# Attention's score rounds back to back, and values' products summed outside the PSUM banks

## The chip, the cores and the metric

The kernel runs on one NeuronCore of a Trainium2 chip. The metric is device time in microseconds (us) of one execution. TensorE (PE) multiplies matrices and writes to PSUM, eight banks of 128 partitions by 512 fp32. VectorE (DVE), ScalarE (ACT) and GpSimd (POOL) work elementwise; the first two read PSUM, and in this kernel GpSimd reads and writes SBUF alone. SyncE (SP) issues the transfers.

## The reference

The program computes two transformer layers, L0 and L1, in fp32 on x of shape (4, 512, 320), with a context of shape (4, 1601, 192). Each layer is

```
h1 = layernorm(x);  x = attention(h1, h1) + x         # 512 keys
h2 = layernorm(x);  x = attention(h2, context) + x    # 1601 keys
h3 = layernorm(x);  a, g = split(h3 @ ff_w1 + ff_b1)
x = (a * gelu(g)) @ ff_w2 + ff_b2 + x
```

where attention has 20 heads of 16 columns:

```
q, k, v = x @ wq, ctx @ wk, ctx @ wv      # per head
a = softmax(q k^T * 16**-0.5)             # over the keys
out = (a v, heads side by side) @ wo + bo
```

## The kernel before

**Units.** The work is cut into units. An attention unit is one layer, one kind (self or cross), one of the four batches and one group of four heads: 20 self units and 20 cross units per layer, 80 in all. A feed-forward unit ("ff") is one layer and batch. Units are in the order self, cross, ff. Keys are taken in chunks of 128: four in a self unit, 13 in a cross unit (the last has 65 keys), so there are 680 chunks.

**A chunk.** The function `main` works on one unit. For each head of a chunk, `score` multiplies the transposed keys (`kT`, 32 partitions per head: 16 of the head, one that adds the negated maximum, the rest zero) by the queries with their maxima (`qT`), into a bank `st` of 128 keys by 512 queries. ScalarE takes the exponential of it into a tile `pr` in SBUF. `values` then multiplies `pr` by the values (`vals`, 16 columns and a column of ones, 17 in all, so that the softmax's sum comes out as well). The four heads' products stand at partitions 0, 32, 64 and 96 of one bank, `av`, and are summed over the unit's chunks inside that bank. After the last chunk ScalarE copies `av` to a tile `o`, and `divide` transposes it and divides by the sums.

**Maxima.** The maxima over the keys must be known before a unit starts. `max_pairs` multiplies queries and keys once more the other way round (`sps`), and VectorE reduces each bank to one column (`pm`, or `nmax` where there is just one stretch of keys). `max_reduce` and `max_end` put these together: the latter transposes the maxima and adds them to the queries, which makes `qT`. Maxima of the next two units are worked on while the current one runs: `give` hands out which.

**Rounds.** A matmul of a score or of a maximum has 32 rows, so four of them with different heads go side by side on TensorE. `round_of` issues two scores (heads 0 and 1, or 2 and 3) and two maxima of the other two heads. A chunk has an even round (heads 0 and 1) and an odd one (2 and 3). An fp32 matmul shows as two passes in the profile, so a round is eight MATMUL lines there.

**Steps.** All other work of TensorE is cut into steps, which wait in queues ("chains"): projections of queries, keys and values (`qps`, `kps`, `vps`), the output projection (`ops`), and transposes of normalised rows, context, divided output and undivided output (`hps`, `cps`, `aps`, `dps`). Projections use columns in tiles of 32, as the values' products do; transposes use the whole array. Each step has a cost, a due round and a test of readiness. `steps` runs between rounds: a credit grows each round by the pace that the queues need, and `pick` takes the step with the earliest due round, shifted by `late_by`. Steps of the cost `LIGHT` are work of VectorE alone. A clock counts rounds. The program's order on each engine is what this planning issues; the engines then run it in order and wait for each other by semaphores.

**Order in a chunk before.** Even round; the values of the chunk before (`flush`); steps. Odd round; steps. So something nearly always stands between two rounds.

**Banks.** Three banks `st` for scores in a ring, four banks `m` for maxima and for steps, one bank `av`. The exponentials' tiles `pr` are a ring of eight in SBUF.

**GpSimd.** `to_slots` spreads keys and queries to their 32-partition slots, in two instructions of GpSimd per step; GpSimd also computes the normalisation's inverse root and adds the output bias to x.

Of the kernel before, what the change touches and what calls it, by code (L numbers as in the profile page):

```python
# [9 lines left out]
F32 = mybir.dt.float32  # L10
I32 = mybir.dt.int32
AF = mybir.ActivationFunctionType
ALU = mybir.AluOpType
# [5 lines left out]
H, DH = 20, 16  # L19
# [40 lines left out]
def kernel(ctx: ExitStack, tc: tile.TileContext, x, context, ws, out):  # L60
# [14 lines left out]


    nc = tc.nc
    dma = nc.sync.dma_start
# [7 lines left out]
    dram = ctx.enter_context(tc.tile_pool(name="dram", bufs=1, space=bass.MemoryType.DRAM))  # L86
    ps_st = ctx.enter_context(tc.tile_pool(name="ps_st", bufs=3, space=PSUM))
    ps_m = ctx.enter_context(tc.tile_pool(name="ps_m", bufs=4, space=PSUM))
    ps_av = ctx.enter_context(tc.tile_pool(name="ps_av", bufs=1, space=PSUM))
    ctx.enter_context(tc.manual_schedule())  # L90
# [13 lines left out]

    vals = const.tile([P, NC2, H, VW], F32, name="vals")
    nc.gpsimd.memset(vals, 1.0)

# [19 lines left out]

    av = ps_av.tile([P, N], F32, name="av")
    nc.vector.memset(av, 0.0)


    xs = [const.tile([P, NQ, D], F32, name=f"x{b}") for b in range(B)]

    def load_x(b):
# [4 lines left out]

    wq1, wk1, wv1, wq2, wo1, wo2 = (  # L140
        wpool.tile([P, 3, D], F32, name=n) for n in ("wq1", "wk1", "wv1", "wq2", "wo1", "wo2")
    )
    wk2, wv2 = (wpool.tile([P, 2, D], F32, name=n) for n in ("wk2", "wv2"))
# [35 lines left out]
    def load_self(l):  # L179
        load_norm(l, 0)  # L180
        load_rows(wq1, ws[l]["q1"], DK)
        load_rows(wk1, ws[l]["k1"], DK)
        load_rows(wv1, ws[l]["v1"], DK)
        load_rows(wo1, ws[l]["o1_w"], DK)

    def load_cross(l):
        load_norm(l, 1)
        load_rows(wq2, ws[l]["q2"], DK)
        load_rows(wk2, ws[l]["k2"], CK)
        load_rows(wv2, ws[l]["v2"], CK)  # L190
        load_rows(wo2, ws[l]["o2_w"], DK)

# [68 lines left out]
    chains = {n: deque() for n in ("divide", "project", "norm", "context", "early", "proj", "values")}  # L261
    clock = {"round": 0, "credit": 0.0, "light": -1, "side": None, "odd": False}
    ALIKE = ("project", "early", "proj", "values")
# [25 lines left out]
    def late_by(n):  # L289

        if not clock["side"]:
            return 0
        cost = sum(chains[n][0][0])
        if clock["side"] == "self":
            return 3 if n not in ALIKE else 1 if cost < 0.85 else 0
        return 4 if n in ALIKE and cost < 0.7 else 0

    def pick():  # L300
        heads = [
            (q[0][1] + (late_by(n) if clock["odd"] else -late_by(n)), n)
            for n, q in chains.items()
            if q and q[0][2]() and q[0][3]() and (q[0][0][0] != LIGHT or clock["light"] < clock["round"])
        ]
        return min(heads)[1] if heads else None
# [24 lines left out]

    def steps(odd, whole=False, spent=0.0):


        clock["credit"] = max(-2.0, min(4.0, clock["credit"] + pace()))
        clock["side"] = None if odd is None else "self" if whole else "cross"
        clock["odd"] = bool(odd)
        done = 1 if spent else 0
        while True:
            name = pick()  # L340
            if name is None:
                break
            cost = sum(chains[name][0][0])
            if cost >= 0.1:
                credit = clock["credit"]
                if odd is None:
                    enough = credit >= (3.0 if done else 0.5 * cost)
                elif odd:
                    enough = not done or credit >= (3.0 if done > 1 else 2.0)
                else:  # L350
                    enough = credit >= (3.0 if done > 1 else 1.5 if done else 0.5)
                if not enough:
                    break
                done += 1
            run(name)
            if cost == LIGHT:
                clock["light"] = clock["round"]
        clock["side"] = None
        clock["round"] += 1

# [418 lines left out]
    def add_finish(u):  # L779
# [29 lines left out]
        def project(t, part):  # L809
            wo = wo2 if u.cross else wo1  # L810
            cols = slice(part * D // 2, (part + 1) * D // 2)
            ps = step_bank([P, 512], "ops")
            for k, at, n in DK:
                for f, m in tiles_of(P):
                    nc.tensor.matmul(  # L815
                        ps[f : f + m, : D // 2],
                        lhsT=held["outT"][:n, k, t * P + f : t * P + f + m],
                        rhs=wo[:n, k, cols],
                        start=(k == 0),
                        stop=(k == 2),  # L820
                    )
            nc.vector.tensor_tensor(xs[u.b][:, t, cols], ps[:, : D // 2], xs[u.b][:, t, cols], ALU.add)

        r = clock["round"]
        add("divide", 0.58, divide, r + 4, yes, lambda: clock["round"] > r)
        if u.g == G - 1:
            for k, at, n in DK:
                add(
                    "divide", 0.58, lambda k=k, at=at, n=n: turn(k, at, n), r + 6 + k,
                    lambda: not chains["project"],  # L830
# [12 lines left out]

            add("divide", 0.0, end, r + 8)

# [14 lines left out]
    def main(u, give, nxt):  # L860
# [3 lines left out]
        def score(c, j, pool=ps_st, tag="st"):  # L864
# [12 lines left out]
            return exponential  # L877

        def values(c):
            r = min(P, u.nkeys - c * P)  # L880
            if u.g in (0, 2):
                until(lambda: units[u.i - u.g].vmade[u.g // 2] > c, "values")
            for j, i in enumerate(HEAD):
                nc.tensor.matmul(  # L884
                    av[i * SLOT : i * SLOT + VW, :],
                    lhsT=vals[:r, c, u.g * HG + i, :],
                    rhs=pr.pop((c, j))[:r, :],
                    start=(c == 0),
                    stop=(c == u.nch - 1),
                )  # L890
            u.valued = c + 1
            if c == u.nch - 1:
                u.o = one.tile([P, N], F32, tag="o", name="o")
                nc.scalar.copy(u.o, av)
                add_finish(u)

        halves = 2 * u.nch
        for h in range(halves):
            c, odd = divmod(h, 2)
            rounds = []  # L900
            if nxt is None or nxt.kind == "ff":

                if not odd:

                    round_of(
                        [
                            lambda j=j, ring=ring: score(c, j, *ring)
                            for j, ring in zip(range(HG), ((ps_st, "st"), (ps_m, "m")) * 2)
                        ],
                        [],  # L910
                    )
            else:
                pair, rounds = give(h)
                round_of([lambda j=j: score(c, j) for j in ((2, 3) if odd else (0, 1))], pair)
            if odd:
                u.scored = c + 1
                late.append(lambda c=c: values(c))
            else:
                flush()
            ends = h == halves - 3 and nxt is not None and nxt.kind != "ff"  # L920
            if ends:
                max_end(nxt)
            if rounds or ends:
                clock["light"] = clock["round"]
            if odd:
                steps(True, not u.cross, 0.6 if ends else 0.0)

            start["quad"] = True
            for i, extra in enumerate(rounds):
                if i and next_cost() is not None:  # L930
                    run(pick())
                round_of([], extra)
            start["quad"] = False
            if h == halves - 4 and nxt is not None and nxt.kind != "ff":
                max_reduce(nxt)
                clock["light"] = clock["round"]
            if not odd:
                steps(False, not u.cross)

# [20 lines left out]
    def ff_main(u, give, nxt):  # L960
        done = 0

        def beside(room, n):
# [6 lines left out]
            if done == u.steps - 1 and nxt is not None and nxt.kind != "ff":  # L970
                max_reduce(nxt)
                max_end(nxt)
            steps(None)
            for _ in range(n - 1):
                steps(None, spent=9.0)

# [71 lines left out]
    def after(u):  # L1048
# [4 lines left out]
        if u.b == B - 1 and u.l + 1 < L:  # L1053
            {"self": load_self, "cross": load_cross, "ff": load_ff}[u.kind](u.l + 1)

    def left(v):
# [20 lines left out]
    def giver(u):  # L1077
# [14 lines left out]
        def give(h, alone=False):  # L1092
# [6 lines left out]
            for v in ahead:  # L1099
                total += left(v)  # L1100


                rest = v.start - (7 if alone else 3) - clock["round"]
                if rest > 0:
# [4 lines left out]
            while owed >= 1.0 and any(left(v) for v in ahead) and not (alone and rounds and rest > -4):  # L1109
                hand = [v for v in ahead if left(v) and all(q and at_hand(v, q) for q in v.pairs)]  # L1110
                if not hand and ahead[0].start - 3 - clock["round"] > 1:
                    break
# [15 lines left out]
    load_x(0)  # L1128
    load_self(0)
    load_bias(0, 0)  # L1130
    load_bias(0, 1)
# [72 lines left out]
```

## Time and profile before

The median of three runs is 3605.57 us (3605.49 to 3605.57).

| what | value |
|---|---|
| time of the profiled execution | 3605.48 us |
| its span in the profile | 3603.7 us |
| granted TensorE clock | 1.0 |
| 0 to 45 us (loads, first unit's preparation) | TensorE busy 41.46 us |
| 400 to 1490 us (cross-attention of layer 0) | TensorE busy 1089.71 us, DVE 698.58, ACT 637.53, POOL 245.60 |
| 1490 to 1820 us (mostly feed-forward) | TensorE busy 327.81 us, DVE 80.91, ACT 75.48 |
| score matmuls, line 868 | 5440 passes, 637 ns mean |
| maxima matmuls of 512 keys, line 718 | 5120 passes, 639 ns mean |
| values' matmuls, line 884 | 5440 passes, 598 ns mean |
| exponentials, line 874 | 2720, 595 ns mean |
| copies of `av`, line 894 | 80, 586 ns mean |
| maxima reductions, line 726 | 2560, 685 ns mean |

A line of a group shows the line number of the kernel, the engine, the operation, the tile written and the tiles read, the shape and the count; then the busy time and the mean of one, and the idle time in front of it with what ended that. A line of the timeline shows start, duration of the merged instructions, and what they are. Four matmuls that lie side by side are each counted as busy, and the passes' durations overlap, so TensorE's speed is read from starts and not from durations. PEld is its weight load, which may lie beside a matmul.

### The profile page before, as it was taken

What the parts mean: (1) busy time and instruction counts of PE and PEld (TensorE: products, weight loads), DVE (VectorE), ACT (ScalarE), POOL (GpSimd) and SP (SyncE); (2) the same over time, 40 slices, a digit from 0 to 9 for tenths busy, and PEclk for the clock granted to TensorE, in tenths of its full rate; (3) what the DMA queues carried; (4) which work ended last, traced back from release to release, by engine and by line L of the source; (5) the groups of instructions that cost most, each with busy time, mean ns of one, the idle gap of its engine ahead of it and who ended that gap; (6) DMA issues with size and microseconds to landing.
All of it is one profiled execution on the core that took longest, in us unless ns stands there. A gap on an engine that the chain in (4) does not pass through costs nothing.

```text
span 3603.7 us, 80038 instructions
## 1 busy us (share of the span) xinstructions
PE 3590.4 (100%) x34386; PEld 1479.2 (41%) x34386; DVE 2037.6 (57%) x3699; ACT 1816.0 (50%) x3665; POOL 794.7 (22%) x1676
## 2 busy tenths in 40 slices
PE   9999999999999999999999999999999999999999
PEld 4344443343343343254443444433433333333455
DVE  7665756666666666422256657566666666664221
ACT  4555455655655655611135554556555555556110
POOL 3323321212311312011122233212222222210100
PEclk9999999999999999999999999999999999999999
DMA  4000000000000000000020000000000000000000
GB/s 126 2 10 18 15 11 4 27 2 3 28 2 2 26 2 6 7 1 7 1 70 2 2 3 2 2 15 2 2 15 2 1 15 1 2 1 1 8 8 15
DMA packets 32106, 41.87 MB, mean 12 GB/s; under 512 B 11780, under 2 KB 30216, under 8 KB 30472
## 3 DMA queue, kind: packets, MB, share of 16 engines
q1 hardware_dynamic: 31752, 36.76, 3.6%
q8 instruction: 270, 4.42, 0.5%
q14 instruction: 84, 0.69, 0.1%
HBM read 29.21 MB, written 7.54 MB: 10 GB/s over the span
## 4 chain that ended last, share of the span: by engine, by line
PE 99%; DVE 0%; ACT 0%; issue 0%; DMA 0%; SPq 0%; DVEq 0%
PE st L868 37%; PE av L884 19%; PE fps L986 8%; PE sps L718 5%; PE vps L666 5%; PE kps L618 5%; PE yps L1021 5%; PE ops L815 3%; PE qps L593 3%; PE fps L998 2%; PE sps L733 2%; PE dps L785 1%; PE mps L773 1%; PE hps L427 1%; PE aps L806 1%; PE cps L506 0%
## 5 line engine op out<-in xcount | busy, mean ns | idle before, releaser
L874 ACT ACTIVATE pr<-st 128x512 f32<-128x512 f32 (+1 forms) x2720 | 1472.4, 595 | 1084.9 <-PE sps L718 907.6
L726 DVE TENSOR_REDUCE pm<-sps 128x1 f32<-128x512 f32 x1920 | 1234.2, 685 | 672.1 <-PE sps L718 672.1
L868 PE MATMUL st<-qT,kT 32*128 32x512 f32 (+1 forms) x5440 | 1558.8, 637 | 1.3 <-ACT pr L874 1.3
L718 PE MATMUL sps<-kT,q 32*128 32x512 f32 x5120 | 1467.0, 639 | 0.2 <-DVE kT L542 0.2
L884 PE MATMUL av<-pr,vals 128*17 128x512 f32 (+1 forms) x5440 | 720.1, 598 | 0.0
L868 PEld LDWEIGHTS st<-qT,kT 32*128 32x128 f32 (+1 forms) x5440 | 441.3, 180 | 618.4 <-issue 478.3
L548 POOL TENSOR_SCALAR kT<-kst,keep,ones 64x200 f32<-64x200 f32 (+2 forms) x796 | 413.1, 519 | 629.1 <-ACT kst L628 391.6
L726 DVE TENSOR_REDUCE nmax<-sps 128x1 f32<-128x512 f32 x640 | 409.5, 685 | 246.5 <-PE sps L718 245.3
L548 POOL TENSOR_SCALAR q<-qst,keep,zero 64x128 f32<-64x128 f32 (+1 forms) x476 | 230.2, 484 | 1408.5 <-ACT qst L605 1375.8
L718 PEld LDWEIGHTS sps<-kT,q 32*128 32x128 f32 x5120 | 426.3, 183 | 29.8 <-DVE pm L726 9.5
L884 PEld LDWEIGHTS av<-pr,vals 128*17 128x17 f32 (+1 forms) x5440 | 92.1, 95 | 493.2 <-issue 484.9
L986 PE MATMUL fps<-hT,w 128*128 128x512 f32 x640 | 287.2, 597 | 0.0
L1004 ACT ACTIVATE gl<-fps,b 128x512 f32<-128x512 f32 x80 | 54.8, 687 | 384.9 <-PE fps L998 384.9
L986 PEld LDWEIGHTS fps<-hT,w 128*128 128x128 f32 x640 | 117.2, 190 | 141.9 <-issue 138.5
L666 PE MATMUL vps<-wv,ctxT 96*32 96x192 f32 (+2 forms) x3264 | 153.3, 302 | 0.0
L666 PEld LDWEIGHTS vps<-wv,ctxT 96*32 96x32 f32 (+1 forms) x3264 | 91.4, 109 | 137.6 <-issue 62.1
L618 PE MATMUL kps<-ctxT,wk 96*32 96x200 f32 (+1 forms) x2560 | 140.8, 338 | 0.0
L593 PE MATMUL qps<-hT,wq 112*32 112x128 f32 (+3 forms) x2880 | 129.3, 311 | 2.0 <-ACT hT L434 2.0
L815 PE MATMUL ops<-wo,aT 112*32 112x160 f32 (+1 forms) x3072 | 130.2, 302 | 0.0
L674 ACT COPY vals<-vps 128x128 f32<-128x128 f32 (+3 forms) x272 | 80.2, 295 | 89.3 <-PE vps L666 88.5
L1005 DVE SCALAR_TENSOR_TENSOR hid<-fps,b,gl 128x512 f32<-128x512 f32 x48 | 35.9, 750 | 156.0 <-ACT gl L1004 153.7
L815 PEld LDWEIGHTS ops<-wo,aT 112*32 112x32 f32 (+1 forms) x3072 | 90.8, 110 | 75.2 <-issue 42.8
(80 smaller groups left out, 2074.6 us busy)
## 6 DMA issues: line engine op xcount, KB each, us to landing
ctxT<-ctxT SPq DMA_DIRECT2D x8, 1200.8 KB, 6.9
w<-in_L_xattn_ff_w_dram SPq DMA_DIRECT2D x4, 1280.0 KB, 9.5
ctxin<-in_ctx_dram SPq DMA_DIRECT2D x24, 192.0 KB, 2.5
w<-in_L_xattn_ff_w_dram SPq DMA_DIRECT2D x2, 1600.0 KB, 11.9
out_dram<-x SPq DMA_DIRECT2D x16, 160.0 KB, 1.8
x<-in_x_dram SPq DMA_DIRECT2D x3, 640.0 KB, 9.4
w1r<-in_L_xattn_ff_w_dram SPq DMA_DIRECT2D x4, 320.0 KB, 11.0
wq<-in_L_xattn_q_dram SPq DMA_DIRECT2D x8, 140.0 KB, 2.7
```

The costliest lines, as they stand in the source:

```text
L548: nc.gpsimd.tensor_scalar(to, stage[rows, :w], keep[b][rows], more[rows], ALU.mult, ALU.add)
L593: nc.tensor.matmul(ps[to, :w], lhsT=wq[:n, k, gs], rhs=first.hT[:n, k, at[i] : at[i] + w], start=(k == 0), stop=(k == 2),)
L618: nc.tensor.matmul(ps[to, :w], lhsT=wk[:n, k, gs], rhs=first.kvT[:n, k, c0 : c0 + w], start=(k == 0), stop=(k == len(u.kck) - 1),)
L666: nc.tensor.matmul(ps[f : f + m, at : at + w], lhsT=u.kvT[:n, k, c * P + f : c * P + f + m], rhs=wv[:n, k, h0 * DH : h1 * DH], start=(k == 0),
L718: nc.tensor.matmul(ps, lhsT=u.q[j * SLOT : (j + 1) * SLOT, t * P : (t + 1) * P], rhs=u.kT[j * SLOT : (j + 1) * SLOT, u.k0 + s * 512 : u.k0 ...
L726: return lambda: nc.vector.tensor_reduce(to, ps, AX.X, ALU.max, negate=(ns == 1))
L815: nc.tensor.matmul(ps[f : f + m, : D // 2], lhsT=held["outT"][:n, k, t * P + f : t * P + f + m], rhs=wo[:n, k, cols], start=(k == 0), stop ...
L868: nc.tensor.matmul(st[:r, :], lhsT=u.kT[rows, u.k0 + c * P : u.k0 + c * P + r], rhs=u.qT[rows, :], start=True, stop=True)
L874: nc.scalar.activation(p[:r], st[:r], AF.Exp)
L884: nc.tensor.matmul(av[i * SLOT : i * SLOT + VW, :], lhsT=vals[:r, c, u.g * HG + i, :], rhs=pr.pop((c, j))[:r, :], start=(c == 0), stop=(c ...
L986: nc.tensor.matmul(ps, lhsT=w1[:, k, i * FF + c * P : i * FF + (c + 1) * P], rhs=u.hT[:, k, :], start=(k == 0), stop=False,)
L1021: nc.tensor.matmul(ps[:, :D], lhsT=hid[c][:, t * P : (t + 1) * P], rhs=w2[:, c, :], start=(c == 0), stop=(c == NHC - 1),)
```

## The change

1. `main` now issues both rounds of a chunk in a row (with a tick of the clock between them), then, in the last chunk of a unit, `max_end` for the next unit, then the values of the chunk before, then steps. Extra rounds of maxima follow after the steps. `max_end` was issued after the odd round of the last but one chunk.
2. The values' products of a chunk go to a bank of the ring `st`, which has four banks now; the bank `av` is gone. The products are no longer summed in the bank. The first chunk's are copied by ScalarE to `o`; each later chunk's are copied by ScalarE to a tile `vo` (from the ring of `pr`) and added to `o` by GpSimd. In the last attention unit of a layer VectorE does these copies and sums straight from the bank.
3. The weights of a values' product are 32 columns wide instead of 17, so that all 128 partitions of the bank are written. The columns beyond 17 are those of the next head, and their results are not used.
4. `steps` is called once per chunk instead of twice, takes up to three steps or more by shares of their cost, and prefers steps with column tiles until a transposing one has been taken. Up to two light steps are taken in one call.
5. The division of a unit becomes ready two rounds after its last values, and is due two rounds later.
6. Both output projections use one tile of weights, `wo`, loaded for each phase (`load_out`) instead of two tiles; `o` has two buffers.
7. The maxima of a unit are to be finished two rounds before it starts instead of three.

The core of the diff:

```diff
-    ps_st = ctx.enter_context(tc.tile_pool(name="ps_st", bufs=3, space=PSUM))
+    ps_st = ctx.enter_context(tc.tile_pool(name="ps_st", bufs=4, space=PSUM))
     ps_m = ctx.enter_context(tc.tile_pool(name="ps_m", bufs=4, space=PSUM))
-    ps_av = ctx.enter_context(tc.tile_pool(name="ps_av", bufs=1, space=PSUM))
...
-    vals = const.tile([P, NC2, H, VW], F32, name="vals")
-    nc.gpsimd.memset(vals, 1.0)
+    columns_of = const.tile([P, NC2 * H * VW + SLOT - VW], F32, name="vals")
+    nc.gpsimd.memset(columns_of, 1.0)
+    vals = columns_of[:, : NC2 * H * VW].rearrange("p (c h w) -> p c h w", h=H, w=VW)
...
+    def load_out(l, name):
+        load_rows(wo, ws[l][name], DK)
...
+    def tick():
+        clock["round"] += 1
         clock["credit"] = max(-2.0, min(4.0, clock["credit"] + pace()))
...
+                share = (0.5, 3.0) if beside else (9.0, 9.0) if beside is False else (0.5, 0.75, 1.5)
+                least = cost * share[done] if done < len(share) else 3.0
+                if clock["credit"] < (3.0 if beside is False else least):
                     break
                 done += 1
+                if clock["tiles"] is not None:
+                    clock["tiles"] = name in ALIKE
...
-        add("divide", 0.58, divide, r + 4, yes, lambda: clock["round"] > r)
+        add("divide", 0.58, divide, r + 6, yes, lambda: clock["round"] >= r + 2)
...
+            ps = ps_st.tile([P, N], F32, tag="st", name="av")
             for j, i in enumerate(HEAD):
+                head = (c * H + u.g * HG + i) * VW
                 nc.tensor.matmul(
-                    av[i * SLOT : i * SLOT + VW, :],
-                    lhsT=vals[:r, c, u.g * HG + i, :],
+                    ps[i * SLOT : (i + 1) * SLOT, :],
+                    lhsT=columns_of[:r, head : head + SLOT],
                     rhs=pr.pop((c, j))[:r, :],
-                    start=(c == 0),
-                    stop=(c == u.nch - 1),
+                    start=True,
+                    stop=True,
                 )
             u.valued = c + 1
+
+            if c == 0:
+                u.o = two.tile([P, N], F32, tag="o", name="o")
+                (nc.vector.tensor_copy if last else nc.scalar.copy)(u.o, ps)
+            elif last:
+                nc.vector.tensor_tensor(u.o, ps, u.o, ALU.add)
+            else:
+                vo = prs.tile([P, N], F32, tag="pr", name="vo")
+                nc.scalar.copy(vo, ps)
+                nc.gpsimd.tensor_tensor(u.o, u.o, vo, ALU.add)
             if c == u.nch - 1:
-                u.o = one.tile([P, N], F32, tag="o", name="o")
-                nc.scalar.copy(u.o, av)
                 add_finish(u)
...
+                for odd in range(2):
+                    if odd:
+                        tick()
+                    pair, rounds = give(2 * c + odd)
+                    extra += rounds
+                    round_of([lambda j=j: score(c, j) for j in ((2, 3) if odd else (0, 1))], pair)
+            u.scored = c + 1
+            if not last and c == u.nch - 1:
                 max_end(nxt)
+            flush()
+            late.append(lambda c=c: values(c))
+            steps(None, 1 if extra or c == u.nch - 1 else 2)
...
-                rest = v.start - (7 if alone else 3) - clock["round"]
+                rest = v.start - (7 if alone else 2) - clock["round"]
```

More of the change, by code (lines that the diff above doesn't have):

```diff
@@ L126 @@
     nc.vector.memset(zero, 0.0)
-    av = ps_av.tile([P, N], F32, name="av")
-    nc.vector.memset(av, 0.0)
     xs = [const.tile([P, NQ, D], F32, name=f"x{b}") for b in range(B)]
@@ L137, in load_x @@
             dma(out=xs[b][:, t], in_=src[:, t])
-    wq1, wk1, wv1, wq2, wo1, wo2 = (
-        wpool.tile([P, 3, D], F32, name=n) for n in ("wq1", "wk1", "wv1", "wq2", "wo1", "wo2")
-    )
+    wq1, wk1, wv1, wq2 = (wpool.tile([P, 3, D], F32, name=n) for n in ("wq1", "wk1", "wv1", "wq2"))
+    wo = wpool.tile([P, 3, D], F32, name="wo")
     wk2, wv2 = (wpool.tile([P, 2, D], F32, name=n) for n in ("wk2", "wv2"))
@@ L183, in load_self @@
         load_rows(wv1, ws[l]["v1"], DK)
-        load_rows(wo1, ws[l]["o1_w"], DK)
+    def load_out(l, name):
+        load_rows(wo, ws[l][name], DK)
     def load_cross(l):
@@ L190, in load_cross @@
         load_rows(wv2, ws[l]["v2"], CK)
-        load_rows(wo2, ws[l]["o2_w"], DK)
     def load_ff(l):
@@ L261 @@
     chains = {n: deque() for n in ("divide", "project", "norm", "context", "early", "proj", "values")}
-    clock = {"round": 0, "credit": 0.0, "light": -1, "side": None, "odd": False}
+    clock = {"round": 0, "credit": 0.0, "lights": 0, "tiles": None}
     ALIKE = ("project", "early", "proj", "values")
@@ L289, in late_by @@
     def late_by(n):
-        if not clock["side"]:
+        if clock["tiles"] is None or chains[n][0][0][0] == LIGHT:
             return 0
[L295 to L298, printed above, removed]
+        return 0 if (n in ALIKE) == clock["tiles"] else 3
     def pick():
         heads = [
-            (q[0][1] + (late_by(n) if clock["odd"] else -late_by(n)), n)
+            (q[0][1] + late_by(n), n)
             for n, q in chains.items()
-            if q and q[0][2]() and q[0][3]() and (q[0][0][0] != LIGHT or clock["light"] < clock["round"])
+            if q and q[0][2]() and q[0][3]() and (q[0][0][0] != LIGHT or clock["lights"])
         ]
@@ L330, in next_cost, with steps @@
         return None if name is None else sum(chains[name][0][0])
-    def steps(odd, whole=False, spent=0.0):
+    def tick():
+        clock["round"] += 1
         clock["credit"] = max(-2.0, min(4.0, clock["credit"] + pace()))
-        clock["side"] = None if odd is None else "self" if whole else "cross"
-        clock["odd"] = bool(odd)
-        done = 1 if spent else 0
+    def steps(beside, lights=1):
+        tick()
+        clock["lights"] = lights
+        clock["tiles"] = True if beside is None else None
+        done = 0
         while True:
@@ L344, in steps @@
             if cost >= 0.1:
[L345 to L352, printed above, removed]
+                share = (0.5, 3.0) if beside else (9.0, 9.0) if beside is False else (0.5, 0.75, 1.5)
+                least = cost * share[done] if done < len(share) else 3.0
+                if clock["credit"] < (3.0 if beside is False else least):
                     break
                 done += 1
+                if clock["tiles"] is not None:
+                    clock["tiles"] = name in ALIKE
             run(name)
             if cost == LIGHT:
-                clock["light"] = clock["round"]
-        clock["side"] = None
-        clock["round"] += 1
+                clock["lights"] -= 1
+        clock["tiles"] = None
     def until(test, name):
@@ L809, in project @@
         def project(t, part):
-            wo = wo2 if u.cross else wo1
             cols = slice(part * D // 2, (part + 1) * D // 2)
@@ L828, in add_finish @@
                 add(
-                    "divide", 0.58, lambda k=k, at=at, n=n: turn(k, at, n), r + 6 + k,
+                    "divide", 0.58, lambda k=k, at=at, n=n: turn(k, at, n), r + 8 + k,
                     lambda: not chains["project"],
@@ L842, in end @@
                 add("project", 0.0, lambda: after(u), now + 6 + u.nch * NQ)
-            add("divide", 0.0, end, r + 8)
+            add("divide", 0.0, end, r + 10)
     late = []
@@ L877, in score @@
             return exponential
+        last = nxt is None or nxt.kind == "ff"
         def values(c):
@@ L892, in values @@
             if c == u.nch - 1:
-                u.o = one.tile([P, N], F32, tag="o", name="o")
-                nc.scalar.copy(u.o, av)
                 add_finish(u)
[L897 to L911, printed above, removed]
-            else:
[L913 to L921, printed above, removed]
+        for c in range(u.nch):
+            extra = []
+            if last:
+                round_of(
+                    [
+                        lambda j=j, ring=ring: score(c, j, *ring)
+                        for j, ring in zip(range(HG), ((ps_st, "st"), (ps_m, "m")) * 2)
+                    ],
+                    [],
+                )
+                tick()
+            else:
+                for odd in range(2):
+                    if odd:
+                        tick()
+                    pair, rounds = give(2 * c + odd)
[3 more added lines that the diff above has]
+            if not last and c == u.nch - 1:
@@ L922, in main @@
                 max_end(nxt)
[L923 to L926, printed above, removed]
+            flush()
+            late.append(lambda c=c: values(c))
+            steps(None, 1 if extra or c == u.nch - 1 else 2)
             start["quad"] = True
-            for i, extra in enumerate(rounds):
+            for i, e in enumerate(extra):
                 if i and next_cost() is not None:
@@ L931, in main @@
                     run(pick())
-                round_of([], extra)
+                round_of([], e)
             start["quad"] = False
-            if h == halves - 4 and nxt is not None and nxt.kind != "ff":
+            if not last and c == u.nch - 2:
                 max_reduce(nxt)
-                clock["light"] = clock["round"]
-            if not odd:
-                steps(False, not u.cross)
     ff_read = []
@@ L972, in beside @@
                 max_end(nxt)
-            steps(None)
+            steps(True)
             for _ in range(n - 1):
-                steps(None, spent=9.0)
+                steps(False)
         hc = one.tile([P, 6, N], F32, tag="ctxT", name="hid")
@@ L1054, in after @@
             {"self": load_self, "cross": load_cross, "ff": load_ff}[u.kind](u.l + 1)
+        if u.b == B - 1 and u.kind == "self":
+            load_out(u.l, "o2_w")
+        if u.b == B - 1 and u.kind == "cross" and u.l + 1 < L:
+            load_out(u.l + 1, "o1_w")
     def left(v):
@@ L1110, in give @@
                 hand = [v for v in ahead if left(v) and all(q and at_hand(v, q) for q in v.pairs)]
-                if not hand and ahead[0].start - 3 - clock["round"] > 1:
+                if not hand and ahead[0].start - 2 - clock["round"] > 1:
                     break
@@ L1129 @@
     load_self(0)
+    load_out(0, "o1_w")
     load_bias(0, 0)
```

## The prediction

> **What bounds the kernel now.** I read the page's busy shares, then the chain that ended last, then the costliest groups, and then single chunks in the timeline of TensorE.
>
> ```profile
> PE 3590.4 (100%) x34386; PEld 1479.2 (41%) x34386; DVE 2037.6 (57%) x3699; ACT 1816.0 (50%) x3665; POOL 794.7 (22%) x1676
> ...
> PE 99%; DVE 0%; ACT 0%; issue 0%; DMA 0%; SPq 0%; DVEq 0%
> ...
> L874 ACT ACTIVATE pr<-st 128x512 f32<-128x512 f32 (+1 forms) x2720 | 1472.4, 595 | 1084.9 <-PE sps L718 907.6
> ```
>
> TensorE is busy all the time and is the chain; ScalarE's exponentials wait for it. But overlapping matmuls make "busy" say little: what counts is the distance from one group's start to the next. So here are two ordinary half chunks of cross-attention, each line the start, the duration and the count:
>
> ```profile
> 1007.67 0.66 PE L785 MATMUL dps<-ident,o 128*128 128x128 f32 x4
> 1008.26 0.90 PE L868 MATMUL st<-qT,kT 32*128 32x512 f32 x2
> 1008.48 0.81 PE L718 MATMUL sps<-kT,q 32*128 32x512 f32 x2
> 1008.79 0.80 PE L868 MATMUL st<-qT,kT 32*128 32x512 f32 x2
> 1009.01 0.70 PE L718 MATMUL sps<-kT,q 32*128 32x512 f32 x2
> 1009.64 1.05 PE L884 MATMUL av<-pr,vals 128*17 128x512 f32 x8
> 1010.62 0.70 PE L868 MATMUL st<-qT,kT 32*128 32x512 f32 x2
> 1010.64 0.70 PE L718 MATMUL sps<-kT,q 32*128 32x512 f32 x2
> 1011.16 0.59 PE L868 MATMUL st<-qT,kT 32*128 32x512 f32 x2
> 1011.17 0.59 PE L718 MATMUL sps<-kT,q 32*128 32x512 f32 x2
> 1011.70 0.65 PE L806 MATMUL aps<-ident,on 128*112 128x128 f32 x4
> ```
>
> A round (four 32-row matmuls side by side, two passes each) takes 1.08 from 1010.62 to the next step, but 1.38 from 1008.26 to the values: there the second score and the two maxima behind it start 0.22 late. And here is a chunk in which no step stood between its two rounds, the form that the change gives to every chunk:
>
> ```profile
> 1454.92 0.70 PE L868 MATMUL st<-qT,kT 32*128 32x512 f32 x2
> ...
> 1455.46 0.59 PE L868 MATMUL st<-qT,kT 32*128 32x512 f32 x2
> ...
> 1455.90 1.58 PE L868 MATMUL st<-qT,kT 32*128 32x512 f32 x3
> ...
> 1456.14 1.57 ACT L874 ACTIVATE pr<-st 128x512 f32<-128x512 f32 x3 [1.61 <-PE sps L718]
> ...
> 1456.79 0.18 PEld L868 LDWEIGHTS st<-qT,kT 32*128 32x128 f32 x1 [0.70 <-ACT pr L874]
> ...
> 1457.86 1.05 PE L884 MATMUL av<-pr,vals 128*17 128x512 f32 x8
> ```
>
> It took 2.94. The fourth score (1456.79) waited for the first exponential of the same chunk, which began at 1456.14 and ran 0.59: with three banks in the scores' ring, the fourth score is written where the first was. So two things cost TensorE time: this ring, and the changes between rounds (32-row tiles) and all else.
>
> **Part 1, the fourth scores' bank: about -141 us.** Over all starts of the timeline, an undisturbed round with other work behind it takes 1.071. What single rounds take above that sums to 91 us (162 rounds behind a transposing step and before the values, median 1.383; 420 behind a column-tiled step, median 1.156). The 41 two-round runs take 2.87 to 3.18 where I reckon 1.93 below; that, and some ten longer runs, is another 50 us. With four banks a chunk's four scores have one each, and the wait is only for exponentials of the chunk before. 91+50 = 141.
>
> **Part 2, fewer changes of tiling: about -204 us, net -197.** In the instruction order of the two programs, the runs of 32-row matmuls fall from 1315 to 694, so 621 pairs of boundaries go. Prices: values take 0.983 to a following round (436 cases) and 0.870 to a following column-tiled step (176): entering a round costs 0.113. In the chunk at 1454.92 a next round's first pass starts 0.963 after the first round's, while a round before other work takes 1.071: leaving costs 0.108. And a round's first pass takes 0.534 to the second, the later ones 0.43 (1455.46 to 1455.90; inside the 1.58 of three): the first weights, 0.107, are loaded in the open once per run. So two rounds together take 0.107+4x0.428+0.108 = 1.93 instead of 2x1.071, and 0.113 less is paid before them: 0.328 x 621 = 204 us. The last 0.107 rests on passes of one row group, the others were waiting; without it 137. A step that now follows the values instead of a round is 0.023 shorter (keys 0.79 for 0.81, output 0.93 for 0.954), some 450 of them: -10. Against that, transposing steps now lie between values and column-tiled steps: changes there rise from 101 to 252, 151 x 0.11 = +17.
>
> The Trainium skill, "TensorEngine Tiling (Array Packing)", Key Properties, says that changing the tiling mode drains the engine; "TensorE: Matmul & The Clock Gate", Part 2 (the drain phase), puts a drain at about 128 cycles. As an estimate from that page, 128/2.4 GHz is 0.053 per change and 2x621x0.053 = 66 us, against 0.221x621 = 137 us by the rows. I take the rows.
>
> **Part 3, values into a ring bank, copied and summed outside.** TensorE does the same 680 groups, with 32 weight columns instead of 17: loads of 32 columns take 0.110 (L815), of 17 columns 0.095 (L884). Twice 0.015 in the open at most per group is 20 us, hidden 0: I take +10. ScalarE gains 576+78 copies and loses 80, of 0.586 (the row of L894): 574x0.586 = 336 us, to about 2150. GpSimd gains 576 sums of 128x512. No such row exists; its sums of 128x4 take 0.199 and of 128x320 0.894, a slope of 2.2 ns an element, so 1.32: +758 us, to about 1550. The last units' 24 sums and 2 copies go to VectorE, under 0.75 each by its 128x512 rows. None of that is on TensorE's path if ScalarE keeps up, so I follow one chunk from its first round (0):
> - Exponential 1 starts at 1.22 (1456.14-1454.92) and its bank is free at 1.87 (1456.79). The values want that very bank (five tiles turn in four banks) at 1.93 to 2.03. Margin about 0.1.
> - Exponential 4 takes the `pr` buffer that the values' first matmul is reading (eight tiles on in a ring of eight), so it starts at about 2.03+1.05 = 3.1 and ends at 3.7; the copy of the values ends at 4.25, copies of steps (0.27 to 0.59) behind it at 4.6 to 4.9. The next first exponential is due at 3.6+1.22 = 4.8 with one short step (2.03+0.87+0.11+0.55), 5.4 with two. ScalarE just keeps up; its loop of exponentials 1 to 4, copy and step copies is about 3.3 against 3.6 to 4.4 of TensorE.
> - In the 62 gaps that hold values alone the next round comes at 3.0, and its second half at 4.0 finds the copy of 4.25 and the fourth score's exponential not done: 0.3 each, +19.
> - GpSimd's sum ends near 5.6; the `vo` buffer is wanted again only a chunk later, the division two rounds later, and keys and queries are used three rounds after they are made. A delay of 1.3 is covered; with these gone it would be 1.3 at each of the 318 steps that make keys or queries, 413 us.
>
> **Part 4, the maxima's end one chunk later: +30.** `max_end` moves from the last but one chunk to the last. Its transposes run at 2.03; but on VectorE the addition that makes `qT` (0.681) stands behind four reductions that begin at 1.24 and take 2.58: ready at 4.5 to 4.6. The next unit's first score is behind the transposes (0.59), the values (0.98) and a step. In 13 units no step follows: the score is wanted at 3.6, 1.0 late. In the other 65, about 4.2 with one step and no wait with more: 0.4 late for some 40. 13+16 = 29.
>
> **Part 5, the shared port: +15.** The Trainium skill, "SBUF — State Buffer", Terms, on the shared port pair, says that VectorE's fast two-port operations and GpSimd's lock each other out for a whole instruction, which speaks against more work on GpSimd. The trace shows one: the normalisation of 64 columns took 665 ns and of 320 columns 439. By the rule, 128 such operations may each lose up to a 1.32 sum, 169 us of VectorE; VectorE has about 1.3 idle in a chunk of 4, so I put 0.1 each on the path. Between 0 and 169.
>
> One output-weights tile instead of two: 9 loads are issued at ends of phases, whole phases before their use, behind the old readers. SP's queue holds nothing urgent then; if it did, a 2.7 us load twice. The clock (9 in every slice) and the ff units are as before. 0.
>
> **Sum.** 3603.7 - 141 - 204 - 10 + 17 + 10 + 19 + 30 + 15 = 3339.7. The profiled run took 3605.48, so 1.8 lies outside the span: 3341.5, and the runs' median of 3605.57 agrees with the profiled one. I say 3342.
>
> **Rivals.**
> - The gain is taken back in part: the second round's weights are loaded in the open (+66) and the values wait 0.1 per chunk for exponential 1, whose margin is no larger (+68). For: the margin. Against: 1455.90's passes. 3342+134 = 3476.
> - Only the ring was worth something, and changes of tiling cost what they cost wherever they stand (starts may be shifted by loads): 3342+204-17 = 3529. Against: 0.983 and 0.870 are the same eight matmuls.
> - Slower: ScalarE becomes the bound, at exponential 1. If copies of values and steps make it late by d beyond its 0.1 margin, values, steps and the next round are all late by d. The sum's gain is 264/680 = 0.39 per chunk, so from d = 0.39 on it is slower; at 0.5, 3342+340 = 3682. For: "TensorEngine Tiling (Array Packing)", PSUM Bottleneck: tiling doesn't speed up evacuation, which may then bound. Against: 2150 of 3340 is 64%.
> - Better: none of the 91 of added costs appears: 3251.
>
> **Numbers.** Forecast 0.60, partly taken back 0.22, ring alone 0.06, slower 0.08, better 0.04. The likeliest's own range is 3285 to 3410; the rival of 3476 and the bounds on parts 2 and 5 take it to 3285 to 3490, about 0.82. A difference under 0.2%, 7 us, can't be told from no change here; no case lies there, so faster 0.91, same 0.01, slower 0.08.
>
> **What would show it.** Two rounds from 0 to values in 1.93 to 2.03, with passes 0.43 apart (part 2; 2.14 refutes it); no wait of a fourth score for `pr` (part 1); GpSimd sums near 1.32 and busy near 1550; ScalarE near 2150; waits of TensorE's loads for `qT` near 30 (part 4). Wrong if values' loads wait long for `pr` or rounds for the copies `vo`.

## The result and the profile after

The changed kernel takes 3354.29 us (median of four, 3353.08 to 3355.13) against 3605.53 for the kernel before beside it: a ratio of 0.9303, with a 95% interval of 0.9287 to 0.9319. The forecast was 3342 us, with 3285 to 3490 as the range.

First the page of the changed kernel: busy shares, then the groups that are new or answer to those shown of before (busy us, mean ns, idle us in front and what ended it).

```profile
PE 3315.3 (99%) x34386; PEld 1533.0 (46%) x34386; DVE 2025.8 (60%) x3724; ACT 2062.3 (61%) x4239; POOL 1519.6 (45%) x2252
...
L868 ACT ACTIVATE pr<-st 128x512 f32<-128x512 f32 (+1 forms) x2720 | 1410.2, 601 | 559.9 <-PE sps L713 453.5
...
L899 POOL TENSOR_TENSOR o<-o,vo 128x512 f32<-128x512 f32 x576 | 730.7, 1269 | 1124.2 <-ACT vo L898 1045.1
L882 PE MATMUL av<-pr,vals 128*32 128x512 f32 (+1 forms) x5440 | 729.3, 605 | 3.1 <-ACT pr L868 3.1
...
L882 PEld LDWEIGHTS av<-pr,vals 128*32 128x32 f32 (+1 forms) x5440 | 109.8, 108 | 449.8 <-ACT pr L868 423.4
...
L898 ACT COPY vo<-av 128x512 f32<-128x512 f32 x576 | 348.5, 605 | 47.6 <-PE av L882 47.2
```

GpSimd carries what was reckoned (1520 us where 1550 was put), and ScalarE less: 2062 where 2150 was put, as its exponentials' busy time fell from 1472.4 to 1410.2 while one of them takes 601 ns for 595. Overlapping time counts once, so more of them run back to back. TensorE waits in front of the values' matmuls for 3.1 us in all. The 423.4 us that the values' weight loads wait for `pr` are idle time of the load beside matmuls that run: of 549 runs of two rounds, 512 reach the next work within 0.1 us of the undisturbed 1.93. Then one chunk in the timeline, start and duration first:

```profile
1007.42 0.70 PE L862 MATMUL st<-qT,kT 32*128 32x512 f32 x2
1007.43 0.70 PE L713 MATMUL sps<-kT,q 32*128 32x512 f32 x2
1007.66 1.26 POOL L899 TENSOR_TENSOR o<-o,vo 128x512 f32<-128x512 f32 x1 [0.83 <-ACT vo L898]
1007.95 0.59 PE L862 MATMUL st<-qT,kT 32*128 32x512 f32 x2
1007.97 1.01 PE L713 MATMUL sps<-kT,q 32*128 32x512 f32 x4
1008.40 0.59 PE L862 MATMUL st<-qT,kT 32*128 32x512 f32 x2
1008.58 2.07 ACT L868 ACTIVATE pr<-st 128x512 f32<-128x512 f32 x4 [0.70 <-PE sps L713]
1008.83 0.59 PE L862 MATMUL st<-qT,kT 32*128 32x512 f32 x2
1008.91 2.33 POOL L543 TENSOR_SCALAR kT<-kst,keep,ones 64x200 f32<-64x200 f32 x4
1009.35 1.07 PE L882 MATMUL av<-pr,vals 128*32 128x512 f32 x8
1010.23 0.86 PE L613 MATMUL kps<-ctxT,wk 96*32 96x200 f32 x16
1010.50 0.62 ACT L898 COPY vo<-av 128x512 f32<-128x512 f32 x1
...
1011.02 0.70 PE L862 MATMUL st<-qT,kT 32*128 32x512 f32 x2
...
1011.32 1.27 POOL L899 TENSOR_TENSOR o<-o,vo 128x512 f32<-128x512 f32 x1
```

The four passes of the scores start at 1007.42, 1007.95, 1008.40 and 1008.83: 0.53, then 0.45 and 0.43. Both rounds together take 1.93 to the values at 1009.35, and the values 0.88 to the keys' step. Before, one such chunk with no step between its rounds took 2.94 and a normal one two rounds of 1.08 to 1.38 with a step between.

**Where the time went.** Adding up the distances from each TensorE group's start to the next group's start, before and after, us:

| groups | before | after | difference |
|---|---|---|---|
| runs of rounds (scores and maxima) | 1600.0 in 1315 | 1387.0 in 694 | -213.0 |
| of these, time above an undisturbed run | 146 | 70 | -76 |
| values | 654.8 | 637.6 | -17.2 |
| steps, transposes, maxima's end | 808.8 | 788.5 | -20.3 |
| feed-forward | 512.1 | 512.7 | +0.6 |

An undisturbed run, one that waits for nothing, is 1.071 for one round and 1.929 for two (both medians); 2.787 for three is reckoned from these. The sum, -249.9, is the difference of the spans (3603.7 and 3353.3) to half a microsecond.

### The profile page after: what moved, and what is told of

It is laid out like the page before. It is cut to its first block, busy times and chain, and to the rows that moved or that the text cites. A ratio compares the mean times of both kernels' runs of the same rounds, so it can differ in the third digit from the quotient of the medians.

```text
span 3353.3 us, 81403 instructions
## 1 busy us (share of the span) xinstructions
PE 3315.3 (99%) x34386; PEld 1533.0 (46%) x34386; DVE 2025.8 (60%) x3724; ACT 2062.3 (61%) x4239; POOL 1519.6 (45%) x2252
## 4 chain that ended last, share of the span: by engine, by line
PE 93%; DVE 5%; POOL 1%; ACT 1%; issue 1%; DMA 0%; SPq 0%; POOLq 0%; ACTq 0%; DVEq 0%
PE st L862 22%; PE av L882 19%; PE sps L713 15%; PE fps L984 8%; PE yps L1019 5%; PE kps L613 5%; PE vps L661 5%; PE ops L809 3%; PE qps L588 3%; PE fps L996 2%; DVE pm L721 2%; DVE nmax L721 2%; PE sps L728 2%; PE dps L780 1%; PE hps L422 1%; PE mps L768 1%
## 5 line engine op out<-in xcount | busy, mean ns | idle before, releaser
L868 ACT ACTIVATE pr<-st 128x512 f32<-128x512 f32 (+1 forms) x2720 | 1410.2, 601 | 559.9 <-PE sps L713 453.5
L721 DVE TENSOR_REDUCE pm<-sps 128x1 f32<-128x512 f32 x1920 | 1195.5, 683 | 498.3 <-PE sps L713 496.2
L862 PE MATMUL st<-qT,kT 32*128 32x512 f32 (+1 forms) x5440 | 1354.8, 614 | 22.1 <-DVE qT L772 10.1
L713 PE MATMUL sps<-kT,q 32*128 32x512 f32 x5120 | 1282.2, 617 | 2.3 <-ACT kst L630 1.5
L899 POOL TENSOR_TENSOR o<-o,vo 128x512 f32<-128x512 f32 x576 | 730.7, 1269 | 1124.2 <-ACT vo L898 1045.1
L882 PE MATMUL av<-pr,vals 128*32 128x512 f32 (+1 forms) x5440 | 729.3, 605 | 3.1 <-ACT pr L868 3.1
L862 PEld LDWEIGHTS st<-qT,kT 32*128 32x128 f32 (+1 forms) x5440 | 457.8, 181 | 275.5 <-ACT pr L868 96.4
L713 PEld LDWEIGHTS sps<-kT,q 32*128 32x128 f32 x5120 | 455.0, 183 | 243.6 <-issue 181.1
L898 ACT COPY vo<-av 128x512 f32<-128x512 f32 x576 | 348.5, 605 | 47.6 <-PE av L882 47.2
L882 PEld LDWEIGHTS av<-pr,vals 128*32 128x32 f32 (+1 forms) x5440 | 109.8, 108 | 449.8 <-ACT pr L868 423.4
```

The source lines that it names most:

```text
L713: nc.tensor.matmul(ps, lhsT=u.q[j * SLOT : (j + 1) * SLOT, t * P : (t + 1) * P], rhs=u.kT[j * SLOT : (j + 1) * SLOT, u.k0 + s * 512 : u.k0 ...
L721: return lambda: nc.vector.tensor_reduce(to, ps, AX.X, ALU.max, negate=(ns == 1))
L862: nc.tensor.matmul(st[:r, :], lhsT=u.kT[rows, u.k0 + c * P : u.k0 + c * P + r], rhs=u.qT[rows, :], start=True, stop=True)
L868: nc.scalar.activation(p[:r], st[:r], AF.Exp)
L882: nc.tensor.matmul(ps[i * SLOT : (i + 1) * SLOT, :], lhsT=columns_of[:r, head : head + SLOT], rhs=pr.pop((c, j))[:r, :], start=True, stop= ...
L898: nc.scalar.copy(vo, ps)
```

## The experiments

Each starts from the changed kernel; times of the kernel before beside them were 3605.22 or 3605.38 us. Left untried are a ninth buffer for `pr`, the maxima's end ahead of two reductions, and extra rounds of maxima ahead of the steps.

### Values between the rounds

```diff
...
                     round_of([lambda j=j: score(c, j) for j in ...], pair)
+                    if not odd:
+                        flush()
...
-            flush()
             late.append(lambda c=c: values(c))
...
```

> The changed kernel (3354 us) with one thing moved: the values of the chunk before stand between the two rounds again, all else, the four-bank ring and the sums outside included, as changed. Runs of 32-row matmuls rise from 694 to 1301. My theory (each run of rounds costs 0.113 to enter, 0.107 for weights loaded in the open, 0.108 to leave): 607 x 0.328 = 199 us more, 3553. If the weights are loaded in the open in either order: 607 x 0.221 = 134 more, 3488. If only the ring of banks was worth something: 3354.

Measured: 3667.14 us (ratio 1.0169, 1.0139 to 1.0198), 313 more than the changed kernel and 114 above the highest of the three expectations. By the table's method: runs of rounds 1579.3 us in 1301, of which 129 above undisturbed runs. So the undisturbed part rose from 1317 to 1450, 133 us for 607 runs: 0.219 each, where 0.215 (leaving, and weights in the open) had been put. Values rose by 63.6, for 595 more entries from values to a round: 0.107 each, where 0.113 had been put. The prices hold, and with the steps' 0.023 behind a round make 207 of the 312 us of span. The other some 105 are waits that this order brings in, 59 in rounds and 45 in steps. First the rounds:

```profile
1007.28 1.09 ACT L868 ACTIVATE pr<-st 128x512 f32<-128x512 f32 x2 [0.47 <-PE sps L713]
1007.31 1.29 DVE L721 TENSOR_REDUCE pm<-sps 128x1 f32<-128x512 f32 x2 [1.10 <-PE sps L713]
1007.71 0.70 PE L862 MATMUL st<-qT,kT 32*128 32x512 f32 x2
1007.73 1.02 PE L713 MATMUL sps<-kT,q 32*128 32x512 f32 x2
1008.25 0.59 PE L862 MATMUL st<-qT,kT 32*128 32x512 f32 x2
1008.26 0.92 PE L713 MATMUL sps<-kT,q 32*128 32x512 f32 x2
```

In this timeline of the experiment the scores of the round at 1007.71 run undisturbed (0.70), but the two maxima's passes need 1.02: the second starts about 0.3 late. One short step separates this even round from the odd one before it, and the first of the odd round's reductions, begun at 1007.31, is just ending; the weights of the late maximum load 0.05 after its end. The four `m` banks go round with five tiles per chunk, so the maximum wants the bank that this reduction frees. The trace agrees over the whole span: in the 202 rounds ahead of values that are over 0.1 late, 194 loads of maxima's weights begin within 0.08 of a reduction's end, and 159 loads of scores' weights as soon after an exponential's. All rounds ahead of values together lose 62 us so.

Another 37 us stand in 30 rounds in front of the division's transposes, which wait for GpSimd:

```profile
PE dps L780 <- POOL o L899: 38.8, 40, 2.4
```

The division of a unit comes before GpSimd has added the last values (in the changed kernel such waits of TensorE are 2.3 us). Against these 99 us, the runs of three rounds are gone, which lose 37 in the changed kernel; with small differences elsewhere the net is 59. The 45 us in steps stand for the most part at the ends of units, where values no longer fill the time until `qT` is there: 16 value steps of one size come between `max_end`'s transposes and a round, and 14 of these took 1.56 or 1.57, against 0.57 without a wait.

So the fourth bank and the sums outside, without rounds in a row, are no gain: 3667 against 3605 for the kernel before. (The steps lie as in the changed kernel, not as before.)

### The values' sum in a bank of its own

```diff
-    ps_st = ctx.enter_context(tc.tile_pool(name="ps_st", bufs=4, space=PSUM))
+    ps_st = ctx.enter_context(tc.tile_pool(name="ps_st", bufs=3, space=PSUM))
+    ps_av = ctx.enter_context(tc.tile_pool(name="ps_av", bufs=1, space=PSUM))
...
-                    ps[i * SLOT : (i + 1) * SLOT, :],
+                    av[i * SLOT : (i + 1) * SLOT, :],
...
-                    start=True,
-                    stop=True,
+                    start=(c == 0),
+                    stop=(c == u.nch - 1),
...
+            if c == u.nch - 1:
+                u.o = two.tile([P, N], F32, tag="o", name="o")
+                nc.scalar.copy(u.o, av)
```

(the copies and sums per chunk go).

> The changed kernel with the values' products summed in a bank of their own again (no copies per chunk, no sums on GpSimd) and so three banks for scores; the rounds stay two in a row. My theory: the fourth score waits for the chunk's first exponential, a run of two rounds takes 2.93 instead of 1.93, about 600 runs by 1.0: 3354 + 600 = 3950, slower than the 3606 of the kernel before. If ScalarE's and GpSimd's extra work is what holds the changed kernel, and the ring matters little: 3300 to 3354.

Measured: 3937.05 us (1.0917, 1.0886 to 1.0949), 13 from the 3950 expected. A chunk of it:

```profile
1008.03 0.70 PE L866 MATMUL st<-qT,kT 32*128 32x512 f32 x2
...
1008.56 0.59 PE L866 MATMUL st<-qT,kT 32*128 32x512 f32 x2
...
1009.00 1.52 PE L866 MATMUL st<-qT,kT 32*128 32x512 f32 x3
...
1009.19 1.09 ACT L872 ACTIVATE pr<-st 128x512 f32<-128x512 f32 x2 [2.05 <-PE sps L717]
...
1009.84 0.18 PEld L866 LDWEIGHTS st<-qT,kT 32*128 32x128 f32 x1 [0.64 <-ACT pr L872]
```

The third score runs alone from 1009.00; the fourth score's weights wait until 1009.84 for the exponential begun at 1009.19. Runs of two rounds between a column-tiled step and the values take 2.87 in the median, and runs of rounds 1982.7 us in all, 596 more than with four banks. So two rounds in a row with three banks are a loss of 9% against the kernel before; the fourth bank makes them a gain, and the values' copies outside are what frees it. With the run before this one, neither half of the change pays without the other: 3667 with the bank alone, 3937 with the order alone, 3354 with both.

### Four banks for scores, three for maxima and steps

The same kernel as the last one with `bufs=4` for `ps_st` and `bufs=3` for `ps_m`.

> As the run with a bank of their own for the values' sums, but four banks for scores and three for maxima and steps. My theory: the odd round's second maximum needs the bank of the even round's first, whose reduction begins at 1.24 and ends at 1.9 after the chunk's start, and is wanted at 0.97: again about 1.0 per chunk, 3950, and some more where a step then finds no bank. If maxima can wait at no cost: 3340, without the copies and sums.

Measured: 4010.96 us (1.1122, 1.109 to 1.1154), 61 above the expected 3950, on the side named. Runs of two rounds take 3.04 each:

```profile
1001.67 2.60 DVE L725 TENSOR_REDUCE pm<-sps 128x1 f32<-128x512 f32 x4 [1.48 <-PE sps L717]
...
1002.41 0.29 PEld L717 LDWEIGHTS sps<-kT,q 32*128 32x128 f32 x2 [0.82 <-DVE pm L725]
1002.41 1.12 PE L717 MATMUL sps<-kT,q 32*128 32x512 f32 x2
```

The last maximum of the chunk that began at 1000.42 starts at 1002.41, when the first reduction, begun at 1001.67, has let go of its bank. Eight banks are too few for four scores, four maxima with steps, and a sum that stays.

### The copy made twice

```diff
                 nc.scalar.copy(vo, ps)
+                nc.scalar.copy(vo, ps)
```

> The changed kernel with the copy of each later chunk's values made twice by ScalarE (the same tile written twice): 576 x 0.605 = 348 us more of ScalarE, from 2062 to 2410. The theory that ScalarE just keeps up (a loop of 3.3 against 3.6 to 4.4 of TensorE): the loop becomes 3.9, longer than the chunks with one short step, so about 0.2 to 0.3 in half of the chunks: 3354 + 70 to 110. If ScalarE is already the bound: 3354 + 348 = 3700. If it has room: 3354.

Measured: 3438.75 us (0.9539, 0.9525 to 0.9553), 84 more, inside the 70 to 110. Busy, and what is idle before the exponentials:

```profile
PE 3392.2 (99%) x34386; PEld 1617.6 (47%) x34386; DVE 2024.6 (59%) x3724; ACT 2373.7 (69%) x4815; POOL 1517.0 (44%) x2252
...
L868 ACT ACTIVATE pr<-st 128x512 f32<-128x512 f32 (+1 forms) x2720 | 1412.7, 603 | 369.9 <-PE sps L713 277.2
```

Of 311 us that ScalarE works longer, a quarter reaches the end, with ScalarE only 69% busy: runs of rounds take 79 us more. In the changed kernel ScalarE has room, but less than one more 0.6 copy per chunk. Why the rounds come late is not settled by this run: the second copy also holds the values' bank 0.6 longer, and in the 181 runs of two rounds that are over 0.1 late, 158 loads of scores' weights begin within 0.08 of the second copy's end. A longer hold of the bank and a later ScalarE are both in the 84.

### Without GpSimd's sums

```diff
                 nc.scalar.copy(vo, ps)
-                nc.gpsimd.tensor_tensor(u.o, u.o, vo, ALU.add)
```

> The changed kernel without GpSimd's sums: the later chunks' values are copied by ScalarE and left out of the result. GpSimd's busy time falls from 1520 to about 790. Theory that the sums lie beside other work and cost only by locking VectorE's normalisations out (put at 15 us, bounds 0 and 169): 3354 - 15 = 3339. If the sums hold nothing: 3354. If keys and queries come late behind them: 3300 or less.

Measured: 3342.24 us (0.9272, 0.9258 to 0.9286), 12 less, near the 15 expected. GpSimd falls from 1519.6 to 793.9 us, and 726 us of its work were worth 12 to the end: 7.6 in runs of rounds, 3.6 in values, 1.7 in steps. The normalisations of 320 columns took 518 ns in the changed kernel, 470 here and 439 in the kernel before, in the direction of the port rule that the prediction cites, but 96 x 0.048 is only 5 us of VectorE. The 64-column ones, whose 665 ns before the prediction took for such a lock, go the other way: 596 ns with the sums and 598 without. How the 12 divide between the port and waits for the sums isn't separated.

### A second sum behind each

```diff
                 nc.gpsimd.tensor_tensor(u.o, u.o, vo, ALU.add)
+                nc.gpsimd.tensor_tensor(vo, u.o, vo, ALU.add)
```

> The changed kernel with a second addition of GpSimd behind each sum (its result goes to the copy's own tile and is used by nothing): GpSimd rises from 1520 to about 2250. If the sums are covered by the margins of two to three rounds: 3354 to 3365. If GpSimd's queue delays keys and queries: up to 318 steps by 1.27, 3354 + 400.

Measured: 3678.94 us (1.0209, 1.0192 to 1.0226), 325 more: neither end as argued. The longest waits name the place (us, times, longest):

```profile
DVE pm L721 <- PE sps L713: 700.6, 618, 4.1
POOL o L899 <- ACT vo L898: 628.8, 300, 8.7
ACT pr L868 <- POOL vo L900: 540.7, 395, 5.7
PEld av L882 <- ACT pr L868: 431.6, 572, 3.2
```

Exponentials wait 540.7 us for the new sums, and the chain that ended last goes through GpSimd for a fifth of the span, where the changed kernel has 1%:

```profile
PE 68%; POOL 21%; ACT 4%; issue 4%; DVE 3%; POOLq 0%; DMA 0%; SPq 0%; ACTq 0%; DVEq 0%
```

It isn't a late key or query; it is a buffer. While the second rounds of a chunk run, eight `pr` tiles are alive: four of this chunk, four of the one before, whose values come only afterwards. The copy `vo` of the chunk before these is a ninth. The ring has eight, so the chunk's last exponential must take the buffer of `vo`, and waits until GpSimd has added it. In the changed kernel's program 572 exponentials, each the fourth of its chunk, carry a wait on GpSimd; there it costs ScalarE 18 us in all, since the sum ends first:

```profile
L899 POOL TENSOR_TENSOR o<-o,vo x576: 1260/1267/1374, 40.6 to 3040.3; 128x512 f32<-128x512 f32 x192
...
  ACT pr L868: 18.4, 19
```

(the changed kernel's answer for line 899: its durations, and who waited for it.) The chunk shown above tells how near it is: a keys' step is four instructions, 2.33 us from the first to the last, and a sum 1.27. The two stand nearly without a break from 1007.66 to 1011.24, in the 3.66 from this sum to the next (busy: 3.29), while GpSimd's share over the span is 45%. With a second sum it would be 4.9 for a chunk that takes 3.60. Such a chunk leaves GpSimd no room for a second sum.

Two things besides are in the 325. The second sum reads and writes `vo` and so holds it for 1.27 more even where GpSimd has time; the run doesn't part this from a GpSimd without time left. And the granted clock was 0.990 in this profile, where the changed kernel's was 0.999: some 76 us of the span at half clock, which can account for 38 us at most.

### VectorE adds straight from the bank

```diff
-            elif last:
+            elif True:
                 nc.vector.tensor_tensor(u.o, ps, u.o, ALU.add)
```

> The changed kernel with VectorE adding each chunk's values straight from the bank to the sum, for all units (the way the last units of a layer do it): 576 copies of ScalarE and 576 sums of GpSimd go, 576 additions of VectorE of about 0.68 to 0.75 come, 390 to 430 us: VectorE's busy time rises from 2026 to about 2440. A chunk of VectorE is then 2.6 + 0.7 + 0.5 = 3.8 against TensorE's 3.6 to 4.4, so some maxima wait for a bank: 3354 + 30 to 120. If GpSimd's part is what costs the changed kernel time: below 3340.

Measured: 3362.31 us (0.9323, 0.9296 to 0.9351), 8 above the changed kernel, where 30 to 120 had been expected; the intervals overlap. What VectorE's sums cost and what GpSimd's absence gives (12 in the run without sums) are both in the 8.

```profile
PE 3329.2 (99%) x34386; PEld 1570.9 (47%) x34386; DVE 2351.7 (70%) x4300; ACT 1784.1 (53%) x3663; POOL 796.4 (24%) x1676
...
L895 DVE TENSOR_TENSOR o<-av,o 128x512 f32<-128x512 f32 x600 | 408.3, 680 | 34.2 <-PE av L882 33.9
```

VectorE has room for 408 us of sums. So it is the bank, not GpSimd's help, that the change lives on: with one engine's work in place of two, the time is the same to about 0.2%.

## Why the prediction was right

- **The mechanism and the size.** Two causes were named, the fourth score's bank and the boundaries of runs, and both are there. Undisturbed runs became 137 us shorter (1454 to 1317) where leaving and weights in the open were put at 621 x 0.215 = 134. The choice to take the 0.107 of weights, which rested on passes of one row group, was right: 1.93 for two rounds, not 2.04. One reading was off a little: by the rows of the chunk at 1454.92 the next round's first pass comes 0.98 after the first's (1455.90), where 0.963 was put, so leaving is nearer 0.09 than 0.108. The time of both rounds, which the sum needs, came as put.
- **Against the drain estimate.** 66 us were the estimate for entering and leaving from the page "TensorE: Matmul & The Clock Gate", 137 the rows'. The values-between run moved 607 runs and found 0.219 and 0.107 per boundary, so the rows' prices hold, and 0.053 a change doesn't. That a change of tiling mode drains TensorE, as the Trainium skill says in "TensorEngine Tiling (Array Packing)", Key Properties, agrees with a cost at each change; how much is 0.1 us each way here.
- **Part 1 was too large by 46.** Of waits above undisturbed runs, 122 us were to go (141, less 19 that were left for the gaps with values alone); 76 went, from 146 to 70. 37 of the 70 are in 17 runs of three rounds: an extra round of four maxima, ahead of two rounds with two maxima each, takes 4.76 or more where 2.79 would do. The sum had no such term. In it, six more maxima want banks whose reductions are still to come; the trace agrees, as 49 weight loads in these runs begin within 0.08 of a reduction's end, but no run moved the extra rounds. The other 33 are spread.
- **Parts 2 and 4 outside the rounds.** Values and steps fell by 37.5, where -23 was put: -70 for entering, -10 for steps behind values, +17 for transposing steps, +10 for the wider weights and +30 for `qT`. Values to a column-tiled step went from 0.870 to 0.883, 9 us for 680. The wait for `qT` was smaller: units' ends lose 13 us more than before, 8 of them in the 13 units without a step, where the values take 1.64 in the mean to the next round for 1.02. The sign and the place were right, and the half of it put on units with one step was too much.
- **Part 3's margins.** Right that ScalarE keeps up (2062 us, 3.1 us of TensorE's wait before values, and the copy-twice run's 84 us inside the 70 to 110 that a 3.3 loop gave, though the longer hold of the bank is in it too). Wrong in its second and last points. The fourth exponential doesn't wait for the values' matmul: in the chunk shown, four exponentials beginning at 1008.58 take 2.07 together, without a gap. The count of eight tiles on took the pool for a strict ring, but buffers pass on when they are free, and the one it gets is `vo`'s. So the cover named for a late sum, "wanted again only a chunk later", is less than a chunk; and a keys' step has four instructions of GpSimd, not the two that the description above says. The second-sum run showed both, at 325 us. That these errors cost the changed kernel only 18 us of ScalarE's time is luck: in the chunk shown the sum ends at 1008.92 and the fourth exponential comes at 1010.03, less than one more sum later.
- **Part 5.** 15 us were put, 12 measured by leaving the sums out, though not all of that need be the port, and the operation of 64 columns that was to show the rule shows nothing of it.

In sum: 42.5 less gained in runs of rounds than the terms that fall there (-213.0 for -255.5), 14.5 more in values and steps. The 15 of part 5 do not come on top, since the table covers the whole difference and what the sums cost lies inside its rows. That leaves 13.6 us of span less than the 264 put, which is why 3354 came and not 3342. That the two are so close is in part luck: the errors of single terms are several times as large and cancel. The slower rival, ScalarE at the first exponential, did not happen; one more copy per chunk costs 84 us, far from the loss that it describes. The partly-taken-back rival, 3476, needed weights in the open, and they aren't.

## What to carry to other kernels

When an engine is 100% busy, read starts, not durations: the price of a boundary between tilings and the late start behind a full ring both hide inside "busy". Putting like work side by side paid here only with a ring as long as the longer run, and a bank that holds a running sum is a bank that the ring lacks; moving the sum out cost two engines 1.0 ms of busy time here (ScalarE 246 us, GpSimd 725) and still won, since neither is on the loop. Count buffers that are alive at one moment, not positions in a ring, to find who waits for whom.

## What the runs showed of the hardware that was not expected

An engine at 45% of the span (GpSimd in the changed kernel) can be nearly full inside a stretch: 3.29 us busy of the 3.66 from one sum to the next, in a chunk with a keys' step. One more 1.27 instruction per chunk, which also holds its buffer longer, cost 325 us, 0.56 for each of 576.
